# Selective scan over four directions: dt times x formed on VectorE's way out of PSUM, one x projection for two directions, and a replanned order of work

## The chip, the cores and the metric

The kernel is one launch on one core of a Trainium2 chip. The metric is device time in microseconds. The program on record takes 24978.93 us, the median of three runs (24968.04 to 24987.69). Everything is fp32.

The core has five engines that the profile names: PE (TensorE, matrix products and transposes, results in PSUM), DVE (VectorE), ACT (ScalarE), POOL (GpSimd, which does not touch PSUM here), and SP, which in this kernel only issues DMAs. Each engine works through its own list in order and waits on semaphores.

## What is computed

Layer 0 is a gated attention over the rows of a 256x256 map of 128 channels, with a residual. Layer 1 is a two-dimensional selective scan, and takes ten elevenths of the time. Its core, cut down from the reference:

```
xz = x @ in_proj_w.T ; xin, z = split(xz)              # 256 channels each
xc = silu(depthwise 3x3 conv of xin)
xs = [rows of xc, columns of xc, rows reversed, columns reversed]   # K = 4 directions, L = 65536
x_dbl = x_proj_w[k] @ xs[k]                            # 8 + 16 + 16 rows: dts_r, B, C
dt = softplus(dt_proj_w[k] @ dts_r + dt_proj_b[k])
for l in range(L):                                     # per direction, 256 channels, 16 states
    h = h * exp(dt[l] * A) + (dt[l] * u[l]) * B[l]
    y[l] = sum over states of h * C[l]
ys = ys + Ds * xs ; the four directions are added back on the map
y = layernorm(y) * norm_g + norm_b ; y = y * silu(z) ; out = x + y @ out_proj_w.T
```

## The kernel before

**Tiling.** The scan goes through the directions in the order 0, 2, 1, 3 (line 813). Each is cut into 64 chunks of four rows, T = 1024 tokens. 256 channels are two halves of 128 partitions. One *unit* is one state of one half of one chunk: 32 units a chunk, 2048 a direction, 8192 in all. Directions 0 and 2 run over rows, 1 and 3 over columns; 2 and 3 run backwards over the same data.

**One unit** (`make_unit`, line 1587). ACT forms the decay exp(dt*A) into a tile `w` (line 1608). The input term dt*x*B comes in two ways. *Turned* (all units but the even states of direction 0): dt*x is held token-major in `dtuT`, and pieces of 128x256 of it are multiplied by the column B in `bT` into a `bx` tile, by ACT (1246) or by POOL (1248); PE transposes eight blocks of it back into the PSUM slot `s` (1628). *Fed* (even states of direction 0): a DMA spreads B over 128 partitions (`b`, 1644), and POOL multiplies it by dt*x in `xu` (1649). DVE runs the scan (1670). A DMA spreads C over 128 partitions (`c`, 1601). The product with C is made by POOL, if the planner sends it there, with the scan's result in SBUF and the carry of the last state on ACT (1695); otherwise by DVE from PSUM, with the carry on DVE (1697, 1688). PE transposes the product and sums it in the PSUM tile `y` (1707). There are two PSUM slots for `s`.

**Once per chunk** (`prep`, line 997). Direction 0 makes xc from the convolution and stores it in `xc_d[0]`. Direction 2 loads it back and turns it to token-major `xs`, stored in `xcT_d`. Direction 1 loads `xs` and turns it to channel-major `xu`, stored in `xc_d[1]`, which direction 3 loads. Every direction then projects x to 40 rows `xd` (1139, ACT evicts at 1145), stores B and C in DRAM (1159), forms dt (PE 1165, ACT 1171), takes its softplus (1183), multiplies x by dt on POOL (1193), turns the product on PE (989) and evicts it on ACT to `dtuT` (993). Direction 3 also finishes the layer: layer norm, gate, output product, residual (1381 to 1574), where the residual is added by DVE as it takes the product out of PSUM (1556).

**The order.** Nothing is scheduled at run time: class `Play` (line 85) plays the program through before it is built. Each task has an engine or a choice of engines, a cost pair from the table `COST` (line 66: time its engine is held, time until its result is there), a due time counted in units, dependencies, and a gate for free buffers. `pick` takes, over all engines, the task that can start first; among an engine's tasks that could start within `close` of the earliest it takes the one due first. `step` emits it. So each engine's list is a result of costs and due times. `choose` (1737) sends a product with C to POOL or DVE by POOL's backlog. The table `TUNE` (857) holds, per direction, the number of buffers of each kind, the leads of the tasks in units, and the constants of `choose`. A DMA on SP was booked as 0.36 us of SP and 7.0 us to its landing.

**Buffers.** 18 tiles of 128x1024 and 12 of twice that are shared by kinds (`w`, `c`, `b`, `hc` and `xu`, `dt`, `dtuT`, `bx`), each with its limit from `TUNE`. The convolution weights `wtap` are reused in direction 3 as the tile `yg`, for the gate.

Of the kernel before, what the change touches and what calls it, by code (L numbers as in the profile page):

```python
# [29 lines left out]
R = 8  # L30
# [30 lines left out]
def _normalise(nc, out, in_, mr):  # L61
# [3 lines left out]
SEM = 0.07  # L65
COST = {
# [3 lines left out]
    "e1024": (0.90, 1.0), "e128": (0.15, 0.25), "xn": (1.25, 1.35), "visit": (4.72, 3.45),  # L70
# [3 lines left out]
    "turn_b": (0.5, 0.65), "dma": (0.36, 7.0), "dma2": (0.72, 7.0),  # L74
    "d512": (0.60, 0.69), "n512": (0.62, 0.81), "t256": (0.34, 0.42), "og": (0.76, 0.85),
    "soft": (0.85, 0.95), "exp2": (0.90, 1.0), "gate": (3.85, 2.60), "bias": (4.54, 4.55),
    "bc": (0.62, 0.70), "four": (0.95, 1.25), "dma3": (1.0, 5.0),
# [3 lines left out]
class Task:  # L81
    __slots__ = ("eng", "cost", "due", "emit", "gate", "left", "ready", "after", "by", "fin", "end")


class Play:
# [4 lines left out]
    def __init__(self):  # L90
        self.free_at = dict.fromkeys(self.ENGINES, 0.0)
        self.avail = {e: [] for e in self.ENGINES}
        self.close = 0.12

# [4 lines left out]
    def task(self, eng, cost, due, emit, deps=(), gate=None, more=0):  # L99

        t = Task()
        t.eng = (eng,) if isinstance(eng, str) else eng
        t.cost = (cost,) if isinstance(cost, str) else cost
        t.due, t.emit, t.gate, t.after, t.by = due, emit, gate, [], None
        t.ready, t.left = 0.0, more
        for d in deps:
            if d.by is None:
                d.after.append(t)
                t.left += 1
            else:  # L110
                t.ready = max(t.ready, self.after_own(d) if t.eng == (d.by,) else d.end + SEM)
        if t.left == 0:
            self.offer(t)
        return t
# [8 lines left out]
    def pick(self):  # L123

        best = None
        for e in self.ENGINES:
            f, can, first = self.free_at[e], [], None
            for t in self.avail[e]:
                r = max(t.ready, f)
# [16 lines left out]
    def step(self):  # L146
# [6 lines left out]
        for x in t.eng:  # L153
            self.avail[x].remove(t)
        t.by, t.fin, t.end = e, now + occupied, now + latency
# [73 lines left out]
def _layer0(tc, ctx, const, ident, gmat, vec, a, x1, x1T):  # L229
# [50 lines left out]
    play = Play()  # L280
    task, sp = play.task, play.sp
# [56 lines left out]
    def job(name, due, pieces, leave, deps=(), cost="e512", eng="ACT", gate=None, first=None):  # L338
# [21 lines left out]
        return task(eng, cost, due, out, (t,))  # L360

    EITHER = {"eng": ("ACT", "DVE"), "cost": ("e512", "d512")}
# [42 lines left out]
    def project(g):  # L405
# [34 lines left out]
        for j in range(BPG // 4):  # L440
# [6 lines left out]
            def scaled(pt, by, j=j):  # L447
# [7 lines left out]
                f"pq_{g}_{j}", U - 3.5 + j, [("mm", product("wq", "xn"))], scaled, [xn[j]],  # L455
# [3 lines left out]
                f"pk_{g}_{j}", U - 3.4 + j, [("mm", product("wk", "kvT"))],  # L459
# [46 lines left out]
        gated = task("ACT", "gate", U - 0.5, sigmoid, [g0, g1])  # L506
# [12 lines left out]
    def row(i):  # L519
# [23 lines left out]
        def scores(t):  # L543
# [16 lines left out]
            "PE", "four", i, scores, [w["q"][r // 2], w["k"][r // 2]], free_heads  # L560
# [29 lines left out]
        for h in range(H):  # L590
# [5 lines left out]
                "ACT", "exp2", i + 0.4 + 0.1 * h, exponent(h), [softs[h]], z["sum"].gate  # L596
# [15 lines left out]
        bc = task("POOL", "bc", i + 1.1, spread, [inv], z["bc"].gate)  # L612
# [15 lines left out]
        for h in range(H):  # L628
            leaves.append(job(
                f"pT_{i}_{h}", i + 0.9 + 0.1 * h, [("turn4", turn(h))],  # L630
# [60 lines left out]
        for j in range(BPG // 4):  # L691
            flips.append(job(
                f"x1p_{g}_{j}", i + 2.6 + 0.2 * j, [("turn4", turned(lambda: w["x1t"].tile, j))],
# [4 lines left out]
                "DVE", "d512", i + 3.0 + 0.2 * j,  # L698
# [11 lines left out]
    with tc.manual_schedule():  # L710
        n_groups, n_rows = 0, 0
        while True:
# [3 lines left out]
            while n_rows < RG * n_groups and scored >= n_rows - 4:  # L716
                row(n_rows)
                n_rows += 1
# [6 lines left out]
def _layer1(tc, ctx, const, dram, ident, vec, mr, a, x1, x1T, out):  # L725
# [18 lines left out]
    xpw = const.tile([P, K, ND, R + 2 * ST], F32, tag="xpw", name="xpw")  # L744
# [9 lines left out]
    with tc.tile_pool(name="l1w", bufs=2) as wp, tc.tile_pool(name="l1wps", bufs=4, space=PSUM) as wps:  # L754
# [22 lines left out]
        for j in range(ND):  # L777
            transposed(woT[:, j, :], oraw[:, j * P : (j + 1) * P], C)
            for k in range(K):
                transposed(xpw[:, k, j, :], xraw[:, k, j * P : (j + 1) * P], R + 2 * ST)  # L780
# [15 lines left out]
    bcd = ctx.enter_context(tc.tile_pool(name="l1bcd", bufs=3, space=DRAM))  # L796
# [34 lines left out]
    def at(u):  # L831
# [3 lines left out]
        return i, p, g, j, g * GS + m, m  # L835

    def turned(i, n):

        return work[i][0] != 0 or n % 2 == 1
# [11 lines left out]
    def direction():  # L851
# [7 lines left out]
            w=7, hc=3, c=3, b=3, xu=3, dt=2, dtuT=1, bx=5, pull=(1.2, 0.15, 0), most=4, fills=1.5,  # L859
            calm=1, close=0.2, piece=-3, decay=-0.3, feed=-2, fill=-3, times=2.2, add=2.5, carry=0.4,  # L860
            early=0.0, conv=(-40.0, 4.5, 0.5), side=3,
        ),
        1: dict(
            w=5, hc=4, c=5, b=3, xu=1, dt=2, dtuT=1, bx=8, pull=(-0.3, 1.5, -1), most=12, fills=5.5,
            calm=2, close=0.2, piece=-9.0, decay=-2, feed=-2, fill=-1.3, times=1.2, add=2.5, carry=1.2,
            early=0.0, conv=(-40.0, 4.5, 0.5), side=5,
        ),
        2: dict(
            w=7, hc=3, c=4, b=3, xu=1, dt=2, dtuT=1, bx=8, pull=(-0.3, 1.5, -1), most=3.0, fills=5.5,
            calm=0, close=0.2, piece=-9.0, decay=-2, feed=-2, fill=-1.3, times=1.2, add=4, carry=1.2,  # L870
            early=0.0, conv=(-40.0, 4.5, 0.5), side=5.0,
        ),
        3: dict(
            w=5, hc=3, c=6, b=3, xu=1, dt=2, dtuT=1, bx=8, pull=(-0.3, 1.5, -1), most=12.0, fills=5.5,
            calm=0, close=0.08, piece=-9.0, decay=-2, feed=-2, fill=-1.3, times=1.6, add=4, carry=0,
            early=0.0, conv=(-40.0, 4.5, 0.5), side=5.0,
# [4 lines left out]
    def room(kind, n=1):  # L881
# [3 lines left out]
        def gate():  # L885
            most = TUNE[direction()].get(kind, 1)
            if held.get(kind, 0) + 1 > most or not free:
# [5 lines left out]
    class Held:  # L893

        def __init__(self, kind, n, name):
            self.kind, self.n = kind, n
# [8 lines left out]
        def free(self, when):  # L905
            held[self.kind] -= 1
# [6 lines left out]
    class Lazy:  # L913

        def __init__(self, kind, n):
            self.kind, self.n, self.held, self.when = kind, n, None, 0.0
            self.room = room(kind, n)
# [25 lines left out]
        def free(self, when):  # L943
            self.held.free(when)

# [51 lines left out]
    def prep(i):  # L997
# [5 lines left out]
        xu = w["xu"] = Lazy("xu", 2)  # L1003

        def store_xc(t):
            for j in range(ND):
                nc.sync.dma_start(xc_d[o][cc][:, j, :], xu.half[j])

        w["stores"] = []
        if k == 0:  # L1010
# [16 lines left out]
            def shift(t):  # L1027
                if c == 0:
                    nc.gpsimd.memset(xn[:, 0, :], 0.0)
                else:  # L1030
                    nc.gpsimd.tensor_copy(xn[:, 0:2, :], xn[:, LR : LR + 2, :])
# [3 lines left out]
            shifted = task("POOL", "pool_x", U - 45, shift, prev.get("conv", ()))  # L1035
# [41 lines left out]
        elif k == 1:  # L1077
            have = [[], []]
            for hh in range(2):

                def load(t, hh=hh):
                    xts.take()
                    w["xs", hh] = xs = p1.tile([P, 2, NB, D], F32, tag="xt", name=f"xs_{i}_{hh}")
                    load_tokens(xs, xcT_d, 1, cc * LR + 2 * hh, cc * LR + 2 * hh + 2)

                loaded = sp(U - 38 + 4 * hh, load, prev["stores"], xts.gate, "dma2")
                for j in range(ND):
                    have[hh].append(turn(
                        lambda j=j, hh=hh: blocks(xu.half[j])[:, 4 * hh : 4 * hh + 4, :],
                        lambda u, j=j, hh=hh: w["xs", hh][:, u // NB, u % NB, j * P : (j + 1) * P],  # L1090
                        f"xsp_{i}_{hh}_{j}", U - 31 + 4 * hh + 1 - j, [loaded], xu.gate, xu.get,
                    ))
                free_after(have[hh], lambda when: xts.give(0, when))
            kept = [sp(U - 18, store_xc, have[0] + have[1], None, "dma2")]
            w["stores"] += kept
        else:

            def load(t):
                xu.get()
                for j in range(ND):  # L1100
                    nc.sync.dma_start(xu.half[j], xc_d[o][cc][:, j, :])

            loaded = sp(U - 34, load, prev["stores"], xu.gate, "dma2")
            have = [[loaded]] * 2
            kept = []
            if k == 2:
                for hh in range(2):

                    def new_xs(hh=hh):
                        if ("xs", hh) not in w:  # L1110
                            xts.take()
                            w["xs", hh] = p1.tile(
                                [P, 2 * NB, D], F32, tag="xt", name=f"xs_{i}_{hh}"
                            )

                    parts = [
                        turn(
                            lambda j=j, hh=hh: w["xs", hh][:, :, j * P : (j + 1) * P],
                            lambda u, j=j, hh=hh: blocks(xu.half[j])[:, 4 * hh + u, :],
                            f"xsp_{i}_{hh}_{j}", U - 25 + 6 * hh + j, [loaded],  # L1120
                            lambda hh=hh: 0.0 if ("xs", hh) in w else xts.gate(), new_xs,
# [3 lines left out]
                    kept += parts  # L1125

                    def store(t, hh=hh):
                        r0 = cc * LR + 2 * hh
                        nc.sync.dma_start(
                            xcT_d[r0 : r0 + 2].rearrange("r (b p) d -> p (r b) d", p=P), w["xs", hh]  # L1130
                        )
                        xts.give(0, t.end)

                    w["stores"].append(sp(U - 22 + 6 * hh, store, parts))
# [3 lines left out]
        def project(j, q):  # L1138
            return lambda pt: nc.tensor.matmul(  # L1139
                pt[0 : R + 2 * ST, :], xpw[:, k, j, :],  # L1140
                xu.half[j][:, q * 512 : (q + 1) * 512], start=j == 0, stop=j == ND - 1,
            )

        def leave_xp(q):
            return lambda pt: nc.scalar.copy(  # L1145
                xd.half[0][0 : R + 2 * ST, q * 512 : (q + 1) * 512], pt[0 : R + 2 * ST, :]
            )

        xds = [
            job(  # L1150
                f"xp_{i}_{q}", U - 22 + q, [("mm", project(j, q)) for j in range(ND)], leave_xp(q),
                have[q], gate=xd.gate, first=xd.get,
            )
            for q in range(QT)
        ]
# [696 lines left out]
```

## Time and profile before

The profiled execution took 24982.69 us, of which 24981.0 us are the span from the first to the last instruction.

| engine | busy us | share of the span | instructions |
|---|---|---|---|
| PE | 23456.4 | 94% | 166196 |
| PEld (weight load, beside PE) | 18229.8 | 73% | 166196 |
| DVE | 23834.6 | 95% | 20642 |
| ACT | 23397.7 | 94% | 44994 |
| POOL | 23426.2 | 94% | 18116 |

| stage, by the first scan of each direction | from us | length us |
|---|---|---|
| attention layer, weights, first chunk | 0.0 | 2159.9 |
| direction 0 | 2159.9 | 5905.2 |
| direction 2 | 8065.1 | 5457.6 |
| direction 1 | 13522.7 | 5340.7 |
| direction 3 and the end | 18863.4 | 6117.6 |

The costliest groups of instructions, as the page lists them:

| line, engine | what | count | busy us | mean ns |
|---|---|---|---|---|
| 1670 DVE | the scans | 8192 | 18864 | 2332 |
| 1688 POOL | product with C | 5760 | 13601.2 | 2374 |
| 1688 DVE | product with C | 2432 | 2959.6 | 1218 |
| 1608 ACT | decays | 8192 | 9315 | 1145 |
| 1246 ACT | pieces of bx | 18761 | 8195.3 | 504 |
| 1248 POOL | pieces of bx | 9911 | 4576.5 | 482 |
| 1707 PE | transpose and sum of the products | 65536 | 8502.5 | 277 |
| 1649 POOL | fed input terms | 1024 | 2427.3 | 2370 |
| 1193 POOL | x times dt | 512 | 1209.7 | 2375 |
| 993 ACT | eviction to `dtuT` | 1024 | 579.3 | 584 |

The DMA queue that SP issues moved 6041.65 MB; 8192 loads of `c` and 1024 of `b`, 512 KB each, are most of it. The granted TensorE clock was 0.986.

How to read it: busy time is the union of the durations of an engine's instructions; neighbours overlap by about 0.1 us, so n instructions in a row take less than n durations. A unit's chain crosses ACT, PE, DVE, POOL and PE again, and tens of units are in flight, so a stage's length is not the length of a chain.

### The profile page before, as it was taken

What the parts mean: (1) busy time and instruction counts of PE and PEld (TensorE: products, weight loads), DVE (VectorE), ACT (ScalarE), POOL (GpSimd) and SP (SyncE); (2) the same over time, 40 slices, a digit from 0 to 9 for tenths busy, and PEclk for the clock granted to TensorE, in tenths of its full rate; (3) what the DMA queues carried; (4) which work ended last, traced back from release to release, by engine and by line L of the source; (5) the groups of instructions that cost most, each with busy time, mean ns of one, the idle gap of its engine ahead of it and who ended that gap; (6) DMA issues with size and microseconds to landing.
All of it is one profiled execution on the core that took longest, in us unless ns stands there. A gap on an engine that the chain in (4) does not pass through costs nothing. (4 is left out here: it accounts for less than half of the span.)

```text
span 24981.0 us, 468784 instructions
## 1 busy us (share of the span) xinstructions
PE 23456.4 (94%) x166196; PEld 18229.8 (73%) x166196; DVE 23834.6 (95%) x20642; ACT 23397.7 (94%) x44994; POOL 23426.2 (94%) x18116
## 2 busy tenths in 40 slices
PE   8999999999999999999999999999999999999998
PEld 6666666666666777777777777777777777777777
DVE  8998999999999999999999999999999999999998
ACT  6888898888988999999999999999999999999998
POOL 5777999999999999999999999999999999999999
PEclk9999999999999999999999999999999999999999
DMA  4325888888888777777777777777776666666665
GB/s 130 89 87 190 304 306 305 303 307 304 305 304 298 261 262 260 261 262 261 261 261 261 251 258 251 258 251 256 252 255 222 210 214 212 210 214 209 213 211 196
DMA packets 2618819, 6072.69 MB, mean 243 GB/s; under 512 B 198113, under 2 KB 1321880, under 8 KB 2616472
## 3 DMA queue, kind: packets, MB, share of 16 engines
q1 hardware_dynamic: 2616184, 6041.65, 71.7%
q8 instruction: 1314, 21.53, 0.4%
q14 instruction: 1033, 8.46, 0.1%
q0 software_dynamic: 288, 1.05, 0.0%
HBM read 5505.04 MB, written 536.87 MB: 242 GB/s over the span
## 5 line engine op out<-in xcount | busy, mean ns | idle before, releaser
L1688 POOL TENSOR_TENSOR hc<-w,c 128x1024 f32<-128x1024 f32 x5760 | 13601.2, 2374 | 684.5 <-DVE w L1670 152.9
L1670 DVE TENSOR_TENSOR_SCAN w<-w,hst,s 128x1024 f32<-128x1024 f32 x5067 | 11578.9, 2329 | 410.5 <-PE s L1628 172.3
L1628 PE MATMUL s<-ident,bx 128*128 128x128 f32 x57344 | 7734.5, 279 | 1128.6 <-DVE w L1670 429.0
L1707 PE MATMUL y<-ident,hc 128*128 128x128 f32 x65536 | 8502.5, 277 | 170.5 <-POOL hc L1688 113.9
L1628 PEld LDWEIGHTS s<-ident,bx 128*128 128x128 f32 x57344 | 6416.9, 142 | 2970.9 <-DVE w L1670 1106.1
L1707 PEld LDWEIGHTS y<-ident,hc 128*128 128x128 f32 x65536 | 7442.1, 142 | 1296.1 <-issue 668.6
L1608 ACT ACTIVATE w<-dt,negA 128x1024 f32<-128x1024 f32 x7168 | 8172.4, 1149 | 162.3 <-PE y L1707 155.9
L1246 ACT ACTIVATE bx<-dtuT,bT 128x256 f32<-128x256 f32 x18761 | 8195.3, 504 | 0.0
L1670 DVE TENSOR_TENSOR_SCAN s<-w,hst,s 128x1024 f32<-128x1024 f32 x2101 | 4893.9, 2336 | 127.7 <-PE s L1628 90.8
L1248 POOL TENSOR_SCALAR bx<-dtuT,bT 128x256 f32<-128x256 f32 x9911 | 4576.5, 482 | 25.1 <-ACT hst L1695 10.5
L1688 DVE TENSOR_TENSOR hc<-s,c 128x1024 f32<-128x1024 f32 x2432 | 2959.6, 1218 | 90.3 <-DMA c<-bc 49.1
L1649 POOL TENSOR_TENSOR w<-xu,b 128x1024 f32<-128x1024 f32 x1024 | 2427.3, 2370 | 14.6 <-DVE hc L1688 12.0
L1052 PE MATMUL cv<-xn,wtap 128*128 128x512 f32 x4608 | 2192.3, 594 | 6.4 <-ACT xn L1039 5.9
L530 POOL TENSOR_TENSOR bias<-tri,mk 128x2048 f32<-128x2048 f32 x256 | 1164.7, 4550 | 642.1 <-DVE nm L568 264.2
L1670 DVE TENSOR_TENSOR_SCAN w<-s,hst,w 128x1024 f32<-128x1024 f32 x693 | 1618.3, 2335 | 81.5 <-POOL w L1649 65.6
L1695 ACT COPY hst<-w 128x1 f32<-128x1 f32 x5760 | 1071.6, 186 | 397.9 <-DVE w L1670 386.8
L1193 POOL TENSOR_TENSOR xu<-dt,xu 128x1024 f32<-128x1024 f32 x512 | 1209.7, 2375 | 52.7 <-ACT dt L1183 52.3
L1608 ACT ACTIVATE s<-dt,negA 128x1024 f32<-128x1024 f32 x1024 | 1142.7, 1116 | 83.0 <-DVE hc L1688 78.4
L1165 PE MATMUL dp<-xd,dtw 8*128 8x512 f32 x2048 | 1155.8, 652 | 26.5 <-ACT xd L1145 22.9
L1052 PEld LDWEIGHTS cv<-xn,wtap 128*128 128x128 f32 x4608 | 776.7, 190 | 512.6 <-issue 505.8
L1139 PE MATMUL xp<-xu,xpw 128*40 128x512 f32 x2048 | 1034.4, 608 | 8.9 <-ACT xu L1070 6.0
L582 ACT ACTIVATE s<-s,nm 128x256 f32<-128x256 f32 x2048 | 1015.7, 501 | 1.3 <-DVE nm L568 0.5
(177 smaller groups left out, 20427.4 us busy)
## 6 DMA issues: line engine op xcount, KB each, us to landing
c<-bc SPq DMA_DIRECT2D x8192, 512.0 KB, 5.4
b<-bc SPq DMA_DIRECT2D x1024, 512.0 KB, 5.5
xc_d<-xu SPq DMA_DIRECT2D x256, 512.0 KB, 5.5
yrow_d<-ys SPq DMA_DIRECT2D x128, 1024.0 KB, 5.4
xu<-xc_d SPq DMA_DIRECT2D x256, 512.0 KB, 6.7
yl<-yrow_d SPq DMA_DIRECT2D x512, 256.0 KB, 5.4
xcT_d<-xs SPq DMA_DIRECT2D x128, 512.0 KB, 3.4
yl<-xc_d SPq DMA_DIRECT2D x128, 512.0 KB, 7.1
```

Of the source, the lines that this page charges most:

```text
L530: nc.gpsimd.tensor_tensor(z["bias"].get(), tri.rearrange("p b h k -> p (b h) k"), w["mk"].tile.rearrange("p (r k) -> p r k", k=N)[:, r : r ...
L1052: return lambda pc: nc.tensor.matmul(pc, wtap[:, j, t, :], xn[:, 2 * q + u : 2 * q + u + 2, v : v + N], start=t == 0, stop=t == 8,)
L1165: return lambda pt: nc.tensor.matmul(pt, dtw[:, k, j, :], xd.half[0][0:R, q * 512 : (q + 1) * 512], start=True, stop=True,)
L1193: nc.gpsimd.tensor_tensor(x, dt.half[j], x, ALU.mult)
L1246: nc.scalar.mul(dst, src, b)
L1248: nc.gpsimd.tensor_scalar(dst, src, b, 1.0, ALU.mult, ALU.mult)
L1608: nc.scalar.activation(dst, w["dt"].half[j], AF.Exp, scale=negA[:, k * ND + j, n : n + 1])
L1628: nc.tensor.transpose(dst[:, x * P : (x + 1) * P], blocks(half)[:, x, :], ident)
L1649: nc.gpsimd.tensor_tensor(box["w"].half[0], w["xu"].half[j], box["b"].half[0], ALU.mult)
L1670: nc.vector.tensor_tensor_scan(rev(states), rev(a), rev(b), hst[k][:, j, n : n + 1], ALU.mult, ALU.add)
L1688: eng.tensor_tensor(box["hc"].half[0], states, box["c"].half[0], ALU.mult)
L1707: nc.tensor.matmul(gr["y"][:, x, :], hc[:, x * P : (x + 1) * P], ident, is_transpose=True, start=gr["fresh"] and x == 4 * q, stop=stop and ...
```

## The change

1. *x times dt.* In directions 2, 1 and 3 POOL's product and ACT's eviction are gone. PE turns dt itself, and DVE multiplies it by token-major `xs` as it takes it out of PSUM, into `dtuT`. Direction 0 is as before. In directions 1 and 2 `xs` lives in `yg` (class `Lent`), in 3 in a shared buffer. Direction 3 loads `xs` from `xcT_d` in place of channel-major x, so direction 1 no longer stores it.
2. *Projection.* Directions 0 and 1 project x with the weights of two directions side by side (80 rows) and store all of it in `xp_d`; directions 2 and 3 load their 24 rows for dt and B from there, and all spread B and C from there.
3. *Kept tiles.* A half's passes alternate in the order of states (0 to 7, then 7 to 0), and in directions 0, 2 and 3 the last three `c` (and `b`) tiles of a pass are used again by the next (`again=3`).
4. *Carries* of units whose product stays on DVE go to ACT in directions 1 and 3 (`last` > 0). The shift of `xn` moves from POOL to ACT, and half the layer-norm scalings may go to POOL.
5. *The planner.* A DMA's landing is now played as a pipe that moves one transfer at a time after a lead; several costs are changed, the output product's pieces among them; an `EITHER` eviction takes its second engine only if that could start over 0.6 us sooner; due times and `TUNE` are changed throughout.

```diff
+LEAD, LAND = 1.5, 1.9
-    "e1024": (0.90, 1.0), "e128": (0.15, 0.25), "xn": (1.25, 1.35), "visit": (4.72, 3.45),
+    "e1024": (0.90, 1.0), "e128": (0.15, 0.25), "xn": (1.25, 1.35), "visit": (4.93, 3.62), "visit1": (4.64, 3.35), ...
-    "turn_b": (0.5, 0.65), "dma": (0.36, 7.0), "dma2": (0.72, 7.0),
+    "turn_b": (0.67, 0.85), "dma": (0.36, 1.6), "dma2": (0.72, 3.2),
...
-                r = max(t.ready, f)
+                r = max(t.ready + t.lag if t.lag and e != t.eng[0] else t.ready, f)
...
+        if e == "SP":
+            self.moved = max(self.moved, now + LEAD) + latency
+            latency = self.moved + LAND - now
...
-        return i, p, g, j, g * GS + m, m
+        n = g * GS + (GS - 1 - m if p % 2 else m)
+        return i, p, g, j, n, m
...
+            def project(j, q):
+                return lambda pt: nc.tensor.matmul(
+                    pt[0 : 2 * KR, :], xpw[:, o, j].rearrange("p h m -> p (h m)"),
+                    xu.half[j][:, q * 512 : (q + 1) * 512], start=j == 0, stop=j == ND - 1,
+                )
...
+            w["stored"] = projected[o, cc] = [sp(U - 16, store_xd, xds)]
...
+                nc.sync.dma_start(xd.half[0][0 : R + ST, :], xp_d[o][cc][KR : KR + R + ST])
...
+            def times_xs(j, q):
+                def leave(pt):
+                    nc.vector.tensor_tensor(
+                        blocks(dtuT.half[j])[:, 4 * q : 4 * q + 4, :],
+                        pt.rearrange("p (u c) -> p u c", c=P), tokens(q)[:, :, j * P : (j + 1) * P],
+                        ALU.mult,
+                    )
...
+            w["scaled"] = [bT, *(
+                job(
+                    f"dtp_{i}_{j}_{q}", U - 14 + 0.5 * (2 * j + q), [("turn4", turn_dt(j, q))],
+                    times_xs(j, q), [w["dts"], *given], "add", "DVE", dtuT.gate, dtuT.get,
+                )
+                for j in range(ND) for q in range(QT)
+            )]
...
-        c_in = linked("c", sp(u - 4, load_c, [w["stored"], *prior("c")], room("c")))
+        if before_u is None:
+            c_in = linked("c", sp(u - 4, load_c, [*w["stored"], *prior("c")], room("c")))
+            box["c_in"] = c_in
+        else:
+            box = boxes[u] = dict(c=None, c_in=None, of=boxes[before_u])
+            c_in = boxes[before_u]["c_in"]
...
-                f"out_{i}_{g}", U + 20 + g, [("turn4", give(g, 0)), ("turn4", give(g, 1))],
+                f"out_{i}_{g}", U + 20 + g, [("mm", give(g, 0)), ("mm", give(g, 1))],
```

For direction 0 `TUNE` goes from w=7, hc=3, c=3, b=3 to w=7, hc=3, c=4, b=2, and its `decay` lead from -0.3 to -0.7 units; for direction 3 from w=5, hc=3, c=6 to w=6, hc=4, c=4; for direction 2 from w=7, c=4 to w=5, c=6.

## The prediction

> **What bounds the kernel now.** I read the busy rows first, cut at the first scan of each direction: the attention layer, then directions 0, 2, 1, 3. Columns: window and its length, then busy us (and instructions) of PE, weight load, DVE, ACT, POOL, then clock, DMA share, GB/s.
>
> ```profile
> 0.00:2159.90 2159.90, 2025.90 (x17836) 1412.50 (x17837) 1841.45 (x6371) 1737.75 (x5265) 1412.16 (x593) 0.99 0.35 98
> 2159.90:8065.10 5905.20, 5666.88 (x31966) 3849.33 (x31964) 5717.82 (x3704) 5237.92 (x8920) 5652.56 (x2649) 0.98 0.87 304
> 8065.10:13522.70 5457.60, 5201.75 (x39143) 4324.54 (x39141) 5231.21 (x2981) 5355.31 (x10314) 5331.59 (x4620) 0.99 0.77 261
> 13522.70:18863.40 5340.70, 4964.71 (x37099) 4079.19 (x37100) 5289.80 (x3071) 5295.29 (x10179) 5256.02 (x4673) 1.00 0.76 254
> 18863.40:24981.00 6117.60, 5597.18 (x40160) 4564.21 (x40157) 5754.29 (x4519) 5771.47 (x10320) 5773.83 (x5584) 0.97 0.64 210
> ```
>
> DVE, ACT and POOL are full together: the fullest of the three is busy 5718 of 5905, 5355 of 5458, 5295 of 5341 and 5774 of 6118 us (97, 98, 99 and 94%). So a stage ends at the sum of work of its fullest engine plus a remainder: 187, 103, 46 and 344 us. The chain that ended last tells only of the last microseconds here. PE's busy time is longer than its work: a 128x128 transpose lasts 277 ns, but eight issued in a row take 0.87 us (0.109 each), so PE has air.
>
> What one instruction costs its engine is the distance to the next start, read from the timeline (start, length, engine, line, operation):
>
> ```profile
> 16007.86 2.33 DVE L1670 TENSOR_TENSOR_SCAN s<-w,hst,s 128x1024 f32<-128x1024 f32 x1
> 16010.23 0.16 DVE L1697 COPY hst<-s 128x1 f32<-128x1 f32 x1
> 16010.31 1.22 DVE L1688 TENSOR_TENSOR hc<-s,c 128x1024 f32<-128x1024 f32 x1
> ...
> 16018.64 13.53 DVE L1670 TENSOR_TENSOR_SCAN w<-w,hst,s 128x1024 f32<-128x1024 f32 x6
> ...
> 16015.66 5.48 POOL L1248 TENSOR_SCALAR bx<-dtuT,bT 128x256 f32<-128x256 f32 x12
> 16021.11 9.35 POOL L1688 TENSOR_TENSOR hc<-w,c 128x1024 f32<-128x1024 f32 x4
> ...
> 16006.25 0.60 ACT L993 COPY dtuT<-dtp 128x512 f32<-128x512 f32 x1
> 16006.73 1.32 ACT L1246 ACTIVATE bx<-dtuT,bT 128x256 f32<-128x256 f32 x3
> ...
> 20154.71 0.69 DVE L1556 TENSOR_TENSOR xt<-xt,out 128x512 f32<-128x512 f32 x1 [0.26 <-PE out L1546]
> 20155.31 0.15 DVE L1697 COPY hst<-s 128x1 f32<-128x1 f32 x1
> ```
>
> A unit (one state, one half of the channels) costs DVE 2.24 us if POOL multiplies by C (six from 16018.64 to 16032.08) and 3.58 if DVE does (16007.86 to the next scan at 16011.44). POOL: a 128x1024 product 2.335, a piece of bx 0.454. ACT: a piece 0.40, an eviction of 128x512 0.48, a carry 0.08. DVE's eviction with a second operand: 0.60 (last two rows).
>
> **The sum of work, part by part.** The planner decides which engine gets what, so I count the built programs' instructions by direction.
>
> (a) *x times dt.* POOL's products xu<-dt,xu go in directions 2, 1, 3: 128, 128, 126 of 2.335 = 299, 299, 294 us. ACT's evictions dtuT<-dtp go: 256, 256, 252 of 0.48 = 123, 123, 121. DVE gets as many evictions with a product: by the nearest row, the residual's eviction of the same shape (0.60), 154, 154, 151. [...] The row has the next start after 0.60, before the 0.69 are over; the row decides. [...]
>
> (b) *One projection for two directions.* 512 matmuls of 0.43 and 256 evictions of xd (0.47: 58 us of ACT in direction 2, as much in 3) go; evictions of 80 rows for 40 cost the same, as 40x512 takes 574 ns and 128x512 takes 584. Matmuls with 80 output rows are in no row: between 0.43 and 0.86, and at the upper end PE merely saves nothing; it hides beside the scan.
>
> (c) *Rebalancing.* With POOL free of (a), the planner sends it 61, 124, 128 and 183 more of the products by C; each takes 1.34 from DVE, puts 2.335 on POOL and 0.08 on ACT. Of bx pieces POOL does 182, 195, 72, 541 fewer (0.454) and ACT 163, 217, 72, 538 more (0.40). In directions 1 and 3 ACT also takes the remaining 383 and 444 carries. The xn shift (62 of 0.57) leaves POOL for ACT; 250 of 512 norms (0.49) leave ACT for POOL (0.454 by the bx piece of the same size).
>
> Busy time plus these, DVE / ACT / POOL:
> direction 0: 5718-82 = 5636 / 5238+101 = 5339 / 5653+142-83-35-5 = 5672;
> direction 2: 5231-166+154 = 5219 / 5355+87+10-123-58 = 5271 / 5332+290-88-299 = 5235;
> direction 1: 5290-172-31+154 = 5241 / 5295+29+41-123 = 5242 / 5256+299-33-299 = 5223;
> direction 3: 5754-245-36+151 = 5624 / 5771+215+50-121-58-123 = 5734 / 5774+427-246-294+114 = 5775.
> The fullest: -46, -84, -53, +1: together **-182**. Direction 3, the slowest, gains nothing in work: POOL stays where it was.
>
> **The waits.** These rows name the part of the remainder that the change reaches (the first two in direction 0, the next three in 2, the last in 3); columns: who waited for what, us in total, times, longest:
>
> ```profile
> POOL hc L1688 <- DMA c<-bc: 101.0, 65, 3.0
> ...
> DVE hc L1688 <- DMA c<-bc: 48.4, 60, 2.1
> ...
> DVE w L1670 <- ACT bx L1246: 72.4, 63, 2.3
> DVE w L1670 <- issue: 39.7, 77, 1.1
> ...
> DVE w L1670 <- ACT hst L1695: 32.6, 20, 1.7
> ...
> DVE xt L1556 <- PE out L1546: 85.4, 94, 13.7
> ```
>
> (d) *Loads.* Direction 0 moves 304 GB/s at 87% DMA; three tiles of c (two of b: one kept) serve the next pass too, so 384 c and 128 b loads of 512 KB go, 268 of 1795 MB. In the old order a c load stands 1.4 (DVE) to 1.9 (POOL) scans ahead of its use, 4 to 5.4 us at 2.88 a scan; in the new one about 4. [...] The DMA view of direction 0 says 6.2 (median of 2047 loads), and 101 us of waits stand on POOL, the fullest engine afterwards. Between 0 and 101 I take **-90**. b's tiles fall from 3 to 2, its lead from 4.4 to 3.8 scans: still over 10 us.
>
> (e) *Decays.* In direction 2 DVE waits 145 us in the three w rows; ACT had done its pieces, so what came late stood behind them: the decays. They stand 1.05 scans ahead of use before and 1.69 after (1.08 and 1.96 in direction 3). Between 0 and -145: **-80**.
>
> (f) *The residual.* The planner now books the out product at twice its old cost; the eight matmuls do take 0.9 us. DVE's 85 us there should mostly go, but POOL is full in direction 3: between 0 and -85, **-60**.
>
> (g) *New waits.* DVE is in order. A product of (a) waits for four PE transposes, issued just ahead, themselves behind PE's adds and feeds; behind it queue the scan, then POOL's product and ACT's carry. Floor: ACT's wait at the same place in direction 2, 5.8 us over 256; ceiling: the residual row, 85.4 over 128 = 0.67 each, 512 us for 768. Direction 3's own ACT wait is 102/252 = 0.4, the others near 0.02; nearest by place is ACT's, so **+45**, about 0.06 each.
>
> (h) *Attention layer.* ACT gets 152 us (473 more e copies of 0.48, fewer others), DVE loses 193, of 1738 and 1841 busy; none bounds it. -80 to +40: **-30**.
>
> SP issues 1280 fewer DMAs; x is kept in a region that only the convolution and the last stage use, free some 19 units before it is needed again: nothing for either.
>
> Sum: -182-90-80-60+45-30 = **-397 us** from the profiled execution (24982.7; span 24981.0): 24586; that lies 4 us above the median of 24978.9, so **24580**.
>
> **Rivals.**
> *Tighter packing (18%)*: directions 0, 2, 3 reach direction 1's 99% full. (5672+5271+5242+5775)/0.991 = 22159 for 22821 now, with (h): 24290. For it: three balanced engines in 2 and 1. Against: 0 fills its pipe at DMA speed, 3 has a tail.
> *Work alone (19%)*: every remainder stays, since another wait was due anyway: -182, about 24795. For it: a full engine's idle times overlap.
> *DVE held by its new evictions (12%)*: at the 0.67 ceiling (g) costs 512, so 24982.7-442+512 = 25050, slower. It decides from 442/768 = 0.58 us a product. For it: the same form of instruction stalls so today. Against: that stall had a mis-sized booking; this turn is booked at its measured 0.45.
> The forecast has 47%, its own range 24430 to 24700.
>
> Within 0.2% (50 us, what can't be told from no change) 4%. **Faster 84%, slower 12%.** The range 24260 to 24880 takes in the tighter packing, and work alone with some of (g); the DVE case stays out.
>
> **What would show it.** (a): xu<-dt,xu only in direction 0; dtuT from DVE near 0.60 apart and its wait for dtp under 0.1 us each; above 0.5 the slow rival is right. (d): DMA under 80% in direction 0 and the two c waits under 30 us. (e): the w waits of direction 2 halved. (f): xt's wait under 30. (c): POOL busy near 5775 in direction 3, whose length falls least in proportion to its remainder. Wrong if directions 2 and 1 don't shorten, or if the attention layer moves over 80 us.

## The result and the profile after

The changed kernel takes 24745.84 us (median of four runs, 24725.31 to 24753.32), the kernel before 24983.31 beside it (24968.04 to 25002.74). The ratio is 0.9903, 95% interval 0.9886 to 0.992: faster by 237 us, where 399 were forecast. The profiled execution took 24753.32 us, its span is 24751.6, its clock 0.982 (0.986 before).

The busy rows of the changed kernel, cut at the same places as those of before and with the same columns:

```profile
0.00:2140.50 2140.50, 2008.52 (x17832) 1394.76 (x17832) 1666.58 (x6050) 1870.39 (x5587) 1420.78 (x592) 0.99 0.34 99
2140.50:8063.50 5923.00, 5742.90 (x31957) 3968.10 (x31956) 5652.90 (x3589) 5347.45 (x9196) 5666.38 (x2460) 0.95 0.75 259
8063.50:13380.30 5316.80, 4974.28 (x38645) 4277.57 (x38644) 5193.14 (x2989) 5259.37 (x10278) 5223.85 (x4424) 0.99 0.69 229
13380.30:18726.10 5345.80, 4977.73 (x37099) 4086.75 (x37097) 5234.16 (x2688) 5230.15 (x10503) 5224.84 (x4600) 1.00 0.72 244
18726.10:24752.00 6025.90, 5300.51 (x39644) 4460.93 (x39644) 5687.36 (x3961) 5720.20 (x10856) 5789.49 (x5351) 0.98 0.54 180
```

The three busy columns of DVE, ACT and POOL are where the forecast put them (direction 0: 5653, 5347, 5666 for 5636, 5339, 5672; direction 3: 5687, 5720, 5789 for 5624, 5734, 5775). The lengths are not:

| stage | before | after | change | forecast |
|---|---|---|---|---|
| attention layer | 2159.9 | 2140.5 | -19 | -30 |
| direction 0 | 5905.2 | 5923.0 | +18 | -136 |
| direction 2 | 5457.6 | 5316.8 | -141 | -149 |
| direction 1 | 5340.7 | 5345.8 | +5 | -38 |
| direction 3 | 6117.6 | 6025.5 | -92 | -44 |

By the profiled executions the gain is 229 us of the 397 forecast. Directions 0 and 1 fell short by 154 and 43 us, the attention layer and direction 2 by 19 together, and direction 3 did better by 48.

The waits of direction 0 after the change (columns as before: who waited for what, us in total, times, longest) answer to the two c rows:

```profile
DVE s L1787 <- PE s L1741: 136.3, 96, 4.9
...
DVE w L1787 <- PE s L1741: 28.3, 28, 4.8
...
DVE hc L1805 <- DMA c<-xp_d: 0.3, 1, 0.3
...
POOL hc L1805 <- PE y L1824: 166.5, 62, 4.5
...
ACT dtuT L1034 <- PE dtp L1030: 174.8, 185, 3.0
```

The waits for loads have gone as forecast (48 us on DVE to 0.3; POOL's 101 to no row of that kind). Three waits for PE stand in their place. These are the same three before:

```profile
DVE s L1670 <- PE s L1628: 18.4, 13, 5.5
...
POOL hc L1688 <- PE y L1707: 21.9, 13, 2.8
...
ACT dtuT L993 <- PE dtp L989: 20.8, 27, 1.9
```

The prediction had said that PE has air. The same view of direction 2 after the change answers to the w rows of before (72.4 for bx, 39.7 for issue, 32.6 for the carry):

```profile
DVE w L1787 <- PE s L1741: 72.8, 129, 2.8
DVE w L1787 <- ACT hst L1812: 15.3, 21, 1.1
...
DVE w L1787 <- ACT bx L1335: 5.4, 6, 2.3
...
DVE w L1787 <- issue: 0.5, 1, 0.5
```

and the new product, by the view of its tile in the same direction (duration min/median/max, then start of the first and last):

```profile
L1305 DVE TENSOR_TENSOR dtuT<-dtp,wtap x256: 660/669/691, 8133.9 to 13354.9; 128x512 f32<-128x512 f32 x128
```

The next DVE instruction starts 0.58 us after it (median of all 768, by the start times of neighbours). Over directions 2, 1 and 3 DVE waited 3.1 us for its 768 transposes in all.

**Why PE came late.** The clock record of the trace (when the granted clock is full and when half) gives 536 us at half clock in direction 0, in 70 episodes, against 236 us in 40 episodes before. 59 of the 70 begin in unit 15 or 16 of a chunk. One of them, PE's timeline of the changed kernel (start, length, engine, line, operation and tiles, count):

```profile
3392.37 2.74 PE L1183 MATMUL xp<-xu,xpw 128*80 128x512 f32 x6
3394.95 1.04 PE L1741 MATMUL s<-ident,bx 128*128 128x128 f32 x8
3395.82 1.02 PE L1183 MATMUL xp<-xu,xpw 128*80 128x512 f32 x2
3396.68 1.91 PE L1824 MATMUL y<-ident,hc 128*128 128x128 f32 x16
3398.52 3.17 PE L1219 MATMUL dp<-xd,dtw 8*128 8x512 f32 x6
3401.61 1.81 PE L1824 MATMUL y<-ident,hc 128*128 128x128 f32 x8
3403.36 2.07 PE L1219 MATMUL dp<-xd,dtw 8*128 8x512 f32 x2
```

and the busy rows of these microseconds (columns as in the first fence):

```profile
3394.00:3401.00 7.00, 6.93 (x34) 4.08 (x33) 6.14 (x5) 6.69 (x12) 7.00 (x4) 1.00 0.73 276
3401.00:3408.00 7.00, 7.00 (x25) 4.55 (x24) 4.92 (x3) 5.81 (x9) 4.79 (x3) 0.56 1.00 390
3408.00:3415.00 7.00, 7.00 (x50) 5.66 (x49) 6.93 (x7) 6.50 (x8) 6.00 (x3) 0.95 0.60 191
```

PE is busy 6.93 of 7.00 us before the clock halves at 3401.8, so PE was not idle ahead of it. In the last 3.4 us before it PE does almost nothing but six dt matmuls in a row (`dp`), which contract over 8 rows. While the mean clock is 0.56, eight y transposes take 1.81 us for 1.04 elsewhere, and DVE and POOL are down to 4.9 and 4.8 of 7. The new order puts six of a chunk's eight dt matmuls in a row, in 59 of the 64 chunks. Before, they stood in three groups with other work between; the chunk at about the same time:

```profile
3415.84 1.12 PE L1165 MATMUL dp<-xd,dtw 8*128 8x512 f32 x2
...
3417.91 1.98 PE L1165 MATMUL dp<-xd,dtw 8*128 8x512 f32 x4
...
3421.72 1.12 PE L1165 MATMUL dp<-xd,dtw 8*128 8x512 f32 x2
```

So far this is only a suspicion; the next section tries it.

### The profile page after: what moved, and what is told of

Its sections match the earlier page's. It is cut to its first block, busy times and chain, and to the rows that moved or that the text cites. A ratio compares the mean times of both kernels' runs of the same rounds, so it can differ in the third digit from the quotient of the medians.

```text
span 24751.6 us, 464821 instructions
## 1 busy us (share of the span) xinstructions
PE 23003.9 (93%) x165172; PEld 18188.1 (73%) x165172; DVE 23434.1 (95%) x19272; ACT 23427.6 (95%) x46416; POOL 23325.3 (94%) x17424
## 5 line engine op out<-in xcount | busy, mean ns | idle before, releaser
L1805 POOL TENSOR_TENSOR hc<-w,c 128x1024 f32<-128x1024 f32 x6255 | 14726.7, 2376 | 529.5 <-DVE w L1787 195.1
L1787 DVE TENSOR_TENSOR_SCAN w<-w,hst,s 128x1024 f32<-128x1024 f32 x5550 | 12670.6, 2329 | 295.0 <-PE s L1741 143.8
L1335 ACT ACTIVATE bx<-dtuT,bT 128x256 f32<-128x256 f32 x19751 | 8578.3, 502 | 2.8 <-PE s L1741 2.5
L1337 POOL TENSOR_SCALAR bx<-dtuT,bT 128x256 f32<-128x256 f32 x8921 | 4103.7, 483 | 22.6 <-ACT dtuT L1034 5.9
L1787 DVE TENSOR_TENSOR_SCAN s<-w,hst,s 128x1024 f32<-128x1024 f32 x1618 | 3775.7, 2338 | 310.1 <-PE s L1741 205.7
L1805 DVE TENSOR_TENSOR hc<-s,c 128x1024 f32<-128x1024 f32 x1937 | 2366.2, 1223 | 101.6 <-DVE s L1787 27.5
L1812 ACT COPY hst<-w 128x1 f32<-128x1 f32 x6255 | 1138.1, 185 | 276.7 <-DVE w L1787 244.7
L576 DVE CUSTOM_DVE_ANT_0 s<-sp,bias 128x256 f32<-128x256 f32 x2048 | 754.4, 415 | 69.1 <-PE sp L557 61.1
L1787 DVE TENSOR_TENSOR_SCAN s<-s,hst,w 128x1024 f32<-128x1024 f32 x319 | 745.2, 2336 | 67.4 <-POOL w L1762 67.4
```

What stands on the lines that cost most here:

```text
L1335: nc.scalar.mul(dst, src, b)
L1337: nc.gpsimd.tensor_scalar(dst, src, b, 1.0, ALU.mult, ALU.mult)
L1787: nc.vector.tensor_tensor_scan(rev(states), rev(a), rev(b), hst[k][:, j, n : n + 1], ALU.mult, ALU.add)
L1805: eng.tensor_tensor(box["hc"].half[0], states, c_now().half[0], ALU.mult)
L1812: nc.scalar.copy(dst, src)
```

## The experiments

**Contraction rows of the dt matmul, after the change (e1).** The dt weights are padded with zeros to the 80 rows that `xd` has anyway (24 in directions 2 and 3): as many instructions in the same order, the same values, only more rows in the contraction.

```diff
-    dtw = const.tile([R, K, ND, P], F32, tag="dtw", name="dtw")
+    dtw = const.tile([2 * (R + 2 * ST), K, ND, P], F32, tag="dtw", name="dtw")
+    nc.vector.memset(dtw, 0.0)
...
+        dp_rows = 2 * KR if k < 2 else R + ST
...
-                pt, dtw[:, k, j, :], xd.half[0][0:R, q * 512 : (q + 1) * 512],
+                pt, dtw[0:dp_rows, k, j, :], xd.half[0][0:dp_rows, q * 512 : (q + 1) * 512],
```

> The changed kernel with one thing more: the matmul that forms dt contracts over all rows of xd that are loaded (80 in directions 0 and 1, 24 in 2 and 3) with zero weights for the others, in place of 8 rows; as many instructions, in the same order, with the same values. Theory A (PE's half clock took the place of the load waits in direction 0: 536 us at half clock there, in one piece per chunk that begins in the stretch of the x projection and the dt matmuls, against 236 us before the change): if the eight-row matmuls are what the clock counts as idle, the half clock in direction 0 falls under 150 us, DVE's and POOL's waits for PE there fall from 165 and 167 us to under 60 each, the stage shortens from 5923 us by 80 to 150, and the whole comes to 24600 to 24670. Rival B (direction 0 is bound by POOL's 5666 us of work and the order of its list): half clock or not, the stage stays within 30 us and the whole at 24720 to 24760. Rival C (the projection's few output columns are what the clock counts): the half clock stays above 400 us and nothing moves.

Measured: 24528.26 us, ratio to the kernel before 0.9818 (0.9804 to 0.9833). Direction 0, busy row and waits of this kernel:

```profile
2139.30:7884.70 5745.40, 5519.21 (x31946) 3787.67 (x31946) 5636.36 (x3588) 5330.75 (x9193) 5667.41 (x2460) 1.00 0.78 267
```

```profile
DVE s L1790 <- PE s L1744: 2.9, 3, 1.0
...
POOL hc L1808 <- PE y L1827: 3.3, 2, 2.5
...
ACT dtuT L1035 <- PE dtp L1031: 87.4, 180, 0.8
```

DVE, ACT and POOL are as busy as in the changed kernel, within 17 us, and the stage is 178 us shorter (80 to 150 were expected). Half clock is 20 us for 536, and the waits of 136 and 167 us are gone. Against the kernel before, direction 0 is now 160 us shorter, for 136 forecast. For direction 0 the cause is shown: it is the few contraction rows, and not the projection's 80 output columns, which e1 leaves alone.

**The same in the kernel before (e2)**, with 40 rows, the height of `xd` there: does the kernel before pay for this too?

```diff
-                pt, dtw[:, k, j, :], xd.half[0][0:R, q * 512 : (q + 1) * 512],
+                pt, dtw[:, k, j, :], xd.half[0][0 : R + 2 * ST, q * 512 : (q + 1) * 512],
```

> The kernel before with the dt matmul contracting over 40 rows (zero weights for 32) in place of 8. Theory A: its half clock (236 us in direction 0, 318 us in direction 3) shrinks there too, but direction 0 still waits for its loads, so less comes of it: 24983 falls by 40 to 150. Rival B: within 30 us of the kernel before. Rival C: half clock as before.

Measured: 24821.11 us, 0.9935 (0.992 to 0.995), 161 us less than the kernel before, a little more than was expected. Direction 0 has 44 us at half clock for 236, and takes 5837 us for 5905:

```profile
2161.90:7998.60 5836.70, 5585.28 (x31967) 3787.22 (x31965) 5715.84 (x3705) 5237.74 (x8920) 5651.67 (x2649) 1.00 0.88 307
```

So 40 rows took most of it away in that order of work. e1 against e2 is the change with most of the half clock taken out of both: -23, -91, -135, +8, -43 us by stage, 284 in all. Direction 3 still has 207 and 217 us of it.

**24 rows (e8)**, e1 with `dp_rows = R + ST` everywhere.

> The padded run with 24 rows of contraction in every direction in place of 80 in directions 0 and 1. If the clock follows the share of the array that is used, 24 rows lie between: half clock in direction 0 of 100 to 450 us and the whole 24560 to 24700. If a few rows are enough: as with 80, under 60 us and 24530. If 24 are as idle as 8: over 500 us and 24730.

Measured: 24728.07 us, 0.9899 (0.9885 to 0.9912), 526 us at half clock in direction 0, which is as long as in the changed kernel:

```profile
2136.90:8055.60 5918.70, 5737.79 (x31954) 3964.72 (x31952) 5653.14 (x3589) 5347.22 (x9195) 5666.40 (x2460) 0.96 0.76 260
```

In direction 0 24 rows act like 8 (526 us for 536). It also excludes that the padding as such (a larger weight tile, zeros in it) made the gain. No number of rows between 24 and 80 was run in this order; 40 left 44 us in the other one. In direction 2, where at most four of these matmuls stand in a row, half clock fell from 55 us to 7 with 24 rows, in e1 and in e8.

**Kept tiles undone (e3)**: every `c` and `b` is loaded again.

```diff
-again=3
+again=0
```

> The changed kernel without kept tiles: c and b are loaded for every unit (8192 and 1024 loads again), all else planned anew by the same rules. As the prediction had it (step d), the removed loads are worth 90 us in direction 0: the whole comes to about 24835, with 50 to 100 us of waits of POOL for c in direction 0. Rival (the longer lead of the loads, about four scans, does it alone, and fewer loads are worth nothing while PE is late): 24720 to 24770, DMA waits under 30 us.

Measured: 25069.69 us, 1.0034 (1.002 to 1.0048): 324 us slower than the changed kernel, over three times what was expected, with direction 0 +105, direction 2 +161, direction 3 +47. The loads' own rows hardly show it (12.5 us of DMA waits on POOL in direction 0). Half clock is in the way in both kernels (402 us in direction 0 here, 536 there), so the next run leaves it out.

**Padded and kept tiles undone (e7)**, e1 with `again=0`.

> The run without kept tiles once more, with PE at full clock by the padded dt matmul; to be read against the padded run (24528; direction 0 at 5745 us, direction 2 at 5294). If fewer loads are worth something by themselves in direction 0, it stays at 5800 to 5860 there with DMA near 0.87; if the 105 us that direction 0 lost without kept tiles were PE's lateness, it comes within 30 us of 5745. Direction 2 is over 5420 again either way if its loss lies in the buffers.

Measured: 24954.0 us, 0.9989 (0.9982 to 0.9995). Its rows of directions 0 and 2:

```profile
2137.80:8054.70 5916.90, 5581.12 (x31934) 3809.82 (x31934) 5668.45 (x3629) 5310.77 (x9066) 5673.10 (x2547) 1.00 0.88 305
8054.70:13546.20 5491.50, 5010.62 (x38654) 4291.38 (x38655) 5240.85 (x3070) 5150.28 (x9829) 5318.56 (x4792) 0.99 0.77 259
```

In direction 0 the fullest engine is the same (POOL 5673, 5667 in e1), the clock is full in both, and the stage is 171 us longer at a DMA share of 0.88 for 0.78. That is longer than either of the two outcomes that were expected. So kept tiles are worth 171 us there within the new buffers (c=4, b=2). By which path isn't shown: POOL waits only 8.5 us for loads of `c`, and the planner moved a little work too (87 more instructions on POOL, 127 fewer on ACT). They aren't worth that against the kernel before: e7's direction 0 is 80 us longer than e2's, which loads as much with c=3, b=3. In direction 2 (+198) the planner also moved work between ACT and POOL (ACT 5259 to 5150, POOL 5231 to 5319), so loads and buffers aren't told apart there. No run took the loads away with the buffers kept as they were before; that stays open.

**Carries back on DVE in directions 1 and 3 (e4).**

```diff
-last=0.6
+last=0
...
-last=0.3
+last=0
```

> The changed kernel with the carries of DVE's units in directions 1 and 3 back on DVE (827 copies). If moving them to ACT cost direction 1 its gain (ACT stands 112 us there and 204 us in direction 3 in front of such a carry, where before there was next to nothing): direction 1 falls from 5346 to about 5300 and direction 3 by up to 80, the whole to 24620 to 24700. Rival (ACT's waits there are air, and DVE's 0.08 us a copy count): 24750 to 24810.

Measured: 24590.87 us, 0.9843 (0.9828 to 0.9858): 155 us faster than the changed kernel, below the range that was expected, direction 1 by 56, direction 3 by 103. The waits of ACT in direction 1 of the changed kernel:

```profile
ACT hst L1812 <- DVE hc L1805: 111.7, 190, 1.2
```

its waits for a carry's input in the same direction of the kernel before:

```profile
ACT hst L1695 <- DVE w L1670: 1.3, 2, 1.0
```

the waits of direction 3 of the changed kernel:

```profile
DVE s L1787 <- ACT w L1721: 100.6, 61, 1.7
...
POOL wtap L1630 <- ACT hst L1812: 94.3, 58, 2.9
...
ACT hst L1812 <- DVE hc L1805: 204.2, 159, 3.0
```

and of e4 in direction 1:

```profile
POOL hc L1805 <- DVE w L1787: 121.1, 190, 1.2
...
ACT hst L1812 <- DVE w L1787: 2.5, 4, 0.8
```

A carry is 0.08 us of ACT, but ACT stood 111.7 us in direction 1 and 204.2 us in direction 3 in front of carries, until DVE had made what they waited for, and what came behind them in its list, decays among it, stood with them. In direction 3 that comes back to DVE as 100.6 us of waits for a decay (`w`), and to POOL as 94.3 at the gate (`wtap`). In e4 the 112 us of ACT in direction 1 are 2.5, and POOL, then the least full of the three (busy 5152 of 5290), waits instead. The plan differs in more than the carries: with `last` at 0 the planner also gives 180 pieces of bx in direction 1 from POOL to ACT.

**Both (e6)**, e1 with e4.

> Both mends together: dt contracts over the loaded rows with zero weights, and the carries of DVE's units in directions 1 and 3 are DVE's. If the two act in different places (half clock in direction 0, ACT's list in 1 and 3) they add: 218 and 155 us off 24746, 24340 to 24420. If they share a cause, 24450 to 24530.

Measured: 24382.69 us (24373.78 to 24382.95), 0.9759 (0.9745 to 0.9772). The two gains add (24745.84-217.6-155.0 = 24373). This is the fastest of all kernels here. Its rows of directions 1 and 3:

```profile
13183.00:18460.50 5277.50, 4877.68 (x37100) 4093.39 (x37098) 5257.94 (x3072) 5268.10 (x10304) 5143.67 (x4420) 1.00 0.73 247
18460.50:24381.00 5920.50, 5300.43 (x39644) 4496.85 (x39644) 5764.94 (x4403) 5714.87 (x10413) 5781.16 (x5349) 0.98 0.55 183
```

Direction 1 ends 9 us above its fullest engine, direction 3 still 139 above. 283 us of half clock stay in direction 3 (207 in e1). Its 72 episodes begin at other units of the chunk (45 of them in unit 9), and there PE did sit idle: 1.7 to 2.8 of the 3.4 us before each. No run tried to fill these gaps.

**The product on POOL (e5)**: part (a) undone in the new order. ACT takes the turned dt out of PSUM, and POOL multiplies it by token-major x.

```diff
-                    nc.vector.tensor_tensor(
-                        blocks(dtuT.half[j])[:, 4 * q : 4 * q + 4, :],
-                        pt.rearrange("p (u c) -> p u c", c=P), tokens(q)[:, :, j * P : (j + 1) * P],
-                        ALU.mult,
-                    )
+                return lambda pt: nc.scalar.copy(
+                    blocks(dtuT.half[j])[:, 4 * q : 4 * q + 4, :],
+                    pt.rearrange("p (u c) -> p u c", c=P),
+                )
...
+                    nc.gpsimd.tensor_tensor(d, d, x, ALU.mult)
```

> The changed kernel with step (a) undone in its work but not in its form: in directions 2, 1, 3 dt is still turned on PE, but ACT evicts it and POOL multiplies it by token-major x; all else planned anew by the same rules. Per direction POOL gets 299 us back, ACT 123, DVE loses 149. If (a) is what shortened direction 2 (by 141 us), spread over three engines this is 90 us a direction: directions 2, 1 and 3 each 60 to 140 us longer than in the changed kernel, the whole 24950 to 25150. Rival (the new order of decays and leads did it): direction 2 within 30 us of 5317, the whole 24730 to 24830.

Measured: 25613.0 us, 1.0255 (1.0241 to 1.0269): 867 us slower than the changed kernel, +258, +330, +271 in directions 2, 1, 3, beyond what was expected. Directions 2 and 1:

```profile
8064.90:13639.70 5574.80, 5039.76 (x38629) 4363.58 (x38629) 5189.33 (x2939) 5349.74 (x10346) 5323.26 (x4520) 0.98 0.65 219
13639.70:19315.10 5675.40, 5075.66 (x37113) 4202.85 (x37111) 5175.17 (x2496) 5429.37 (x10878) 5329.35 (x4549) 0.98 0.68 229
```

The fullest engine explains 91 and 195 us (ACT 5259 to 5350; DVE's 5234 to ACT's 5429). The rest came with half clock (260, 235 and 606 us in directions 2, 1, 3, for 55, 0 and 232) and waits for PE. That the new due times alone made direction 2's gain is excluded, since e5 keeps those of the other work and is slower there than the kernel before (5575 us for 5458); but it is no clean price of (a), because the clock moved with it.

## Why the prediction was right or wrong

**Right in direction, and the time within its range, which was 620 us wide; the gain 60% of the forecast.** By its steps:

- **The sum of work** held in every stage, within 1.5% for each engine. Its fullest engine in direction 3 stayed where it was, as forecast, and the stage fell by its remainder alone (344 to 236). Of this fall (f) is 71 us. The rest was in no term and is luck: DVE's wait for PE's transposes there (the w row) fell from 142.3 to 27.8 us and half clock from 316 to 232 us, and no run shows why.
- **(a)** The product costs DVE 0.58 us to the next start, for 0.60: the next instruction starts before the product's own 0.67 us are over. The row of the residual was the right neighbour.
- **(g)** New waits for the transposes: 3.1 us for +45, under the floor of 5.8. The slow rival (0.58 us of wait a product) had nothing to stand on.
- **(e)** The w rows of ACT and issue fell from 145 to 21 us. Direction 2 got 141 of 149 us, and 164 with the clock restored (e1); DVE's wait for PE's transposes of bx took back a part: 16.1 to 72.8 us in the w row, though the s row fell from 39.9 to 11.5.
- **(f)** 85.4 to 14.7, as forecast (under 30). **(h)** -19 for -30.
- **(d)**, the step that failed: "Between 0 and 101 I take -90." Its signs came true (DMA at 75% in direction 0, both c waits gone) without the time. The waits for loads did go, and were replaced in the same stage by waits for PE at half clock. Direction 0 gave +18 where -136 stood in the sum; with the dt matmul padded it gave -160 (e1), of which 69 belong to the kernel before's own half clock (e2). With the clock nearly full on both sides (e1 against e2) direction 0 gained 91: 48 are the work of its fullest engine, for 46 forecast, and 43 are left for (d) and the rest of the new order, half of the 90. The prediction shows the clock column (0.98) and made no term of it; "PE has air" was read from durations at full clock.
- **(c)**, the second: the carries of directions 1 and 3 were priced at 0.08 us on ACT and a gain on DVE (-31, -36). They cost 56 and 103 us (e4, whose plan also differs in some pieces of bx), since what such a copy cost ACT was its place in the list (111.7 and 204.2 us of waits in front of it) and not its length. So direction 1 did not shorten (+5), which the prediction had named as a sign of being wrong. It asked who waits behind a waiting instruction for (a) and not for these 827.

Of the rivals, *work alone* (24795, that every remainder stays) is the nearest in time and wrong in how: the remainders of directions 2 and 3 fell by 45 and 108 us, those of 0 and 1 rose by 69 and 66. *Tighter packing* (24290) is what e6 comes near (24383), once the two faults are out.

## What to carry to other kernels

Read the clock in the stretch and not as a mean (0.982 over this kernel, 0.56 in the 7 us shown above): where an engine that is off the bound stands late, look at what PE did just before. Here a new order had moved matmuls over 8 contraction rows together, six in a row, and half clock in that stage went from 236 to 536 us. Zero-padding them to rows that are there anyway cost no instruction in the loop here and gave 218 us. A small copy given to an engine is priced by what stands behind it in that engine's list until its input is ready (0.08 us of work a carry, 56 and 103 us of time here); leave it on the engine that makes its input if that one is not the fuller.

## What was not expected of the hardware

- The granted clock fell to half while PE was busy 6.93 of 7.00 us, after matmuls over 8 rows. A busy PE did not keep the clock full: 8 and 24 rows gave 536 and 526 us at half clock in direction 0, 80 rows 20 us, with as many instructions in the same order. Of the changed kernel's 141 stretches at half clock all but one last 3.413 us or a multiple of it.
- How many of these matmuls stand in a row went with it. In direction 0 of the changed kernel each of the 59 groups of six saw the clock halve within 4.7 us of the group's start. Of the kernel before's 63 groups of four in direction 0, 22 did.
- At half clock a dt matmul lasts longer (1120 ns, the mean of 104 in direction 0 of the changed kernel, for 623 ns at full clock, the mean of 387), and the episodes last 7.7 us on average (536 us over 70).
- Direction 1 has as many dt matmuls over 8 rows and ran without any half clock (0 us of 5346). There they stand in pairs 3 us apart, as PE's timeline of the changed kernel shows:

```profile
16002.25 1.12 PE L1219 MATMUL dp<-xd,dtw 8*128 8x512 f32 x2
...
16005.20 1.12 PE L1219 MATMUL dp<-xd,dtw 8*128 8x512 f32 x2
...
16008.15 1.12 PE L1219 MATMUL dp<-xd,dtw 8*128 8x512 f32 x2
```

That spreading them in direction 0 would do as well as padding is an estimate from this and wasn't tried.
